# Second layer of a graph-attention kernel: partial sums scaled and added straight from PSUM in chains of multiply-add instructions

## Chip, cores, metric

The kernel runs on one core of a Trainium2 chip. The metric is device time in microseconds. Three runs of the kernel before took 3546.62, 3557.57 and 3558.91 us (median 3557.57). Everything below on single instructions comes from one profiled execution.

## What is computed

Four graph layers follow each other on 3327 nodes with 512 features; each one is `x = x + layer(relu(layernorm(x)), adj)`. The first three are attention layers with 8, 4 and 8 heads, the fourth takes a mean over neighbours. The change concerns the second:

```python
def _L1_gnn_ref(H, A, W, a_l, a_r):
    N_HEADS, D_K = 4, 128
    mask = A + jnp.eye(n, dtype=A.dtype) > 0
    Wh = (H @ W).reshape(n, N_HEADS, D_K)
    sl = jnp.einsum('nhd,hd->nh', Wh, a_l)
    sr = jnp.einsum('nhd,hd->nh', Wh, a_r)
    e = jax.nn.leaky_relu(sl[:, :, None] + sr.T[None, :, :], negative_slope=0.2)
    e = jnp.where(mask[:, None, :], e, -jnp.inf)
    alpha = jnp.nan_to_num(jax.nn.softmax(e, axis=2), nan=0.0)
    out = jnp.einsum('nhm,mhd->nhd', alpha, Wh).reshape(n, -1)
    return jax.nn.elu(out)
```

## The kernel before, in words

**Factored softmax.** exp(leaky_relu(s1 + s2)) is exp(s1)·exp(s2) where s1 + s2 > 0, and exp(0.2·s1)·exp(0.2·s2) elsewhere. So the numerator of a row is `c0 · (T0 @ B0) + c1 · (T1 @ B1)`. T0 and T1 are matrices of 0 and 2 (the neighbours with s1 + s2 > 0, and the others). B0 and B1 are the 128 projected features times the exponential of s2, with the exponential itself as a 129th column (DA = 129) that gives the denominator. c0 and c1 are scales per row and head. They are kept in `L.c` (tile `cpm`), which `close_terms` (lines 562 to 600) computes once a layer from the scores of all nodes: VectorE reductions (568 to 570), a transpose on TensorE (572), a small matmul (579) that hands the maxima to all partitions, a dozen short VectorE instructions (581 to 599), and one exponential on ScalarE (600).

**Pieces.** B is fp32 and is used in pieces along the free axis. For the first of the five groups of source nodes (`JG`: 6, 6, 6, 4 and 4 tiles of 128) these are three bf16 pieces, 387 columns, against the fp8 matrix (line 757). For the other groups there are two fp32r pieces, 258 columns, against a matrix that ScalarE (groups 1 and 2, tile `ts`) or VectorE (groups 3 and 4, tile `tv`) casts to fp32r first (`real`, line 634; matmul line 754). All of them add into one accumulator per row tile: a PSUM bank whose columns 0 to 386 hold three partial sums of 129 columns. Somebody has to add the three.

**Order of the work** (`attention`, lines 680 to 830). The loop goes over chunks of four row tiles (the last has two), heads h, a = 0 and 1 for T0 and T1, and passes. A pass takes two row tiles k over all 26 source tiles j: 52 matmuls. There are four accumulators, two for a pass. In the very first head the passes of a = 0 are cut in two: both pairs over the first 22 source tiles, then both over the last 4, so all four accumulators are full at nearly the same time. When a pass ends, VectorE reads its accumulators (line 775: a reduction that adds the three partial sums of one row tile into R[:, k, a, :]). Then `hooks.run` issues a piece of other work: layer norm, projection and score terms of finished tiles for the next layer. After a = 0 line 789 flips T0 to T1 on VectorE. After both a, VectorE multiplies R by the scales (797), adds the two halves (799), divides (801, 802, 804) and writes the output tile A.

VectorE also makes compares (662), masks (669) and the casts of `tv` for the passes to come. The tile framework places the instructions of each engine in an order of its own, within their dependences; each engine then works through its list strictly in order. Buffers that matter: `acc` 4, `tv` 2, `ts` 3, `tht` 10, R 1.

Of the kernel before, what the change touches and what calls it, by code (L numbers as in the profile page):

```python
# [32 lines left out]
ALU = mybir.AluOpType  # L33
AX = mybir.AxisListType
# [3 lines left out]
P = 128  # L38
# [14 lines left out]
def tile_gnn(ctx: ExitStack, tc: tile.TileContext, x, adj, W0, a01, W1, al, ar, W2, a2,  # L53
             Ws, bs, Wn, bn, Wc, bc, out):
    nc = tc.nc
# [49 lines left out]
    def dims(l):  # L105


        H = heads[l]
        DA = D // H + 1
        AO = -(-(3 * DA + 1) // 8) * 8 if l != 1 else 3 * DA + 1  # L110
        return H, DA, AO, 2 * AO

    abd = []
    for l in range(3):
        H, DA, AO, HW = dims(l)
# [446 lines left out]
    def close_terms(L):  # L562

        l = L.l
        H = heads[l]
        s2v = L.s12[:, 1].rearrange("p t h -> p h t")
        ex = pre.tile([P, 2 * H], F32, name="ex", bufs=1)
        nc.vector.tensor_reduce(ex[:, :H], s2v, AX.X, ALU.max)
        nc.vector.tensor_reduce(ex[:, H:], s2v, AX.X, ALU.min)
        nc.vector.tensor_scalar(ex[:, H:], ex[:, H:], -1.0, None, op0=ALU.mult)  # L570
        tp = ps.tile([2 * H, P], F32, name="tp", bufs=2)
        nc.tensor.transpose(tp, ex, ident)
        m = pre.tile([16, 1], F32, name="mx", bufs=1)
        nc.vector.tensor_reduce(m[:2 * H], tp, AX.X, ALU.max)

        dgm = pre.tile([16, 16], F32, name="dgm", bufs=1)
        nc.vector.tensor_scalar(dgm[:2 * H, :2 * H], ident[:2 * H, :2 * H], m[:2 * H], None, op0=ALU.mult)
        pM = ps.tile([P, 2 * H], F32, name="mm")
        nc.tensor.matmul(pM, ones_row[:2 * H, :], dgm[:2 * H, :2 * H], start=True, stop=True)
        M = pre.tile([P, 2 * H], F32, name="M", bufs=1)  # L580
        nc.vector.tensor_copy(M, pM)
        fl = pre.tile([1, 1], F32, name="fl", bufs=1)
        nc.vector.tensor_reduce(fl, M[0:1, :], AX.X, ALU.max)
        nc.vector.tensor_scalar(fl, fl, S2_MAX, None, op0=ALU.is_gt)
        nc.vector.tensor_max(flagf, flagf, fl)
        L.c = pre.tile([P, NT, 2, H], F32, name="cpm")
        Mb = M[:, None, :H].to_broadcast([P, NT, H])
        s1v = L.s12[:, 0]
        uv = pre.tile([P, D], F32, name="e", bufs=1)
        u, v = [uv[:, o:o + NT * H].rearrange("p (t h) -> p t h", h=H) for o in (0, D // 2)]  # L590
        nc.vector.tensor_scalar(u, Mb, SLOPE, None, op0=ALU.mult)
        nc.vector.tensor_scalar(v, s1v, 1.0 - SLOPE, None, op0=ALU.mult)

        nc.vector.tensor_sub(L.c[:, :, 0, :], v, u)
        nc.vector.scalar_tensor_tensor(L.c[:, :, 0, :], Mb, -1.0, L.c[:, :, 0, :], op0=ALU.mult, op1=ALU.min)

        nc.vector.tensor_add(v, v, Mb)
        nc.vector.tensor_max(v, v, u)
        nc.vector.tensor_scalar(L.c[:, :, 1, :], v, -1.0, None, op0=ALU.mult)
        nc.scalar.activation(L.c, L.c, AF.Exp)  # L600
# [79 lines left out]
    def attention(L, hooks, open_next, close):  # L680

        l = L.l
        H, DA, AO, HW = dims(l)
        DK = DA - 1
        masks = mask_tiles(0, l == 1) if l else masks0
        for c, (t0, nt) in enumerate(chunks):
# [3 lines left out]
            for h in range(H):  # L690
# [10 lines left out]
                for a in range(2 if l == 1 else 1):  # L701
                    row = []
                    for g, (_, nj) in enumerate(JG):
                        if l == 1:
# [3 lines left out]
                            v = (tl if two else tl.bitcast(BF16))[:, :nj * w].rearrange("p (j w) -> p j w", j=nj)  # L708
                            ld = nc.sync.dma_start(v.bitcast(F32) if two else v, abd[l][g][h, a])
                        else:  # L710
                            if g in ahead:
                                v = ahead.pop(g)
                            else:
                                v = pieces_tile(L, mp if l else bp, g)
# [21 lines left out]
                R = mp.tile([P, PER, 2, DA], F32, name="R", bufs=1)  # L736
                deg = l == 0 and h == 0
                for a in range(2 if l == 1 else 1):
                    passes = [(range(k0, min(nt, k0 + 2)), range(NT)) for k0 in range(0, nt, 2)]
                    if c == 0 and h == 0 and a == 0:  # L740
                        cut = JG[-1][0]
                        passes = [(ks, range(0, cut)) for ks, _ in passes] + [(ks, range(cut, NT)) for ks, _ in passes]
                    acc = {}
                    for ks, js in passes:
                        thr = {}
                        for j in js:
                            g, jj = jwhere[j]
                            if l == 1 and KIND[g] != "b" and g not in thr:
                                thr[g] = real(a, g, ks, th)
                            for k in ks:  # L750
                                if j == 0:
                                    acc[k] = accs.tile([P, 512], F32, name="acc")
                                if g in thr:
                                    mm = nc.tensor.matmul(acc[k][:, :2 * DA], thr[g][:, k - ks[0], jj, :], ab[a][g][:, jj, :],  # L754
                                                     start=(j == 0), stop=(j == NT - 1), skip_group_check=True)
                                elif l == 1:
                                    mm = nc.tensor.matmul(acc[k][:, :3 * DA], th[a][g][:, k, jj, :], ab[a][g][:, jj, :3 * DA],  # L757
                                                     start=(j == 0), stop=(j == NT - 1), skip_group_check=True)
                                else:
                                    o = 1 if deg else 0  # L760
                                    nc.tensor.matmul(acc[k][:, :3 * DA + o], th[0][g][:, k, jj, :],  # L761
                                                     ab[0][g][:, jj, :3 * DA + o], start=(j == 0), stop=False,
                                                     skip_group_check=True)
                                    mm = nc.tensor.matmul(acc[k][:, AO:AO + 3 * DA + o], th[1][g][:, k, jj, :],  # L764
                                                     ab[0][g][:, jj, AO:AO + 3 * DA + o], start=False, stop=(j == NT - 1),
                                                     skip_group_check=True)
                            if j == JG[3][0]:
                                late = mm.ins.name
                        if l == 2 and last and h == H - 1:
                            load_y2(yp, 0, late)  # L770
                        if js[-1] != NT - 1:
                            continue
                        for k in ks:
                            if l == 1:
                                nc.vector.tensor_reduce(R[:, k, a, :], acc[k][:, :3 * DA].rearrange("p (s d) -> p d s", s=3),
                                                        AX.X, ALU.add)
                            else:
                                v = acc[k][:, :2 * AO].rearrange("p (a w) -> p a w", a=2)[:, :, :3 * DA]
                                nc.vector.tensor_reduce(R[:, k], v.rearrange("p a (s d) -> p a d s", s=3), AX.X, ALU.add)  # L779
                            if deg:  # L780
                                n = pn(t0 + k)
                                nc.vector.tensor_reduce(deg2[:n, t0 + k:t0 + k + 1],
                                                        acc[k][:n, 3 * DA:AO + 3 * DA + 1:AO], AX.X, ALU.add)
                        gone.append(mm.ins.name)
                        hooks.run(1 if last else 3, hook, 2 if hook % 2 and c == 0 or hook % 3 == 0 and c else 1, 2 if last else 1)
                        hook += 1
                    if a == 0:
                        for pu, mu in flip:
                            nc.vector.tensor_tensor(pu, pu, mu, ALU.bitwise_xor)
                        if h == H - 1 and not last:  # L790
                            pending = loops
                if h == H - 1 and not last:
                    set_loops(pending, gone[-2])
                if c == 0 and h == 0:
                    close_terms(L)
                Rv = R[:, :nt]
                nc.vector.tensor_mul(Rv, Rv, L.c[:, t0:t0 + nt, :, h:h + 1].to_broadcast([P, nt, 2, DA]))
                num = R[:, :, 0, :]
                nc.vector.tensor_add(num[:, :nt], Rv[:, :, 0, :], Rv[:, :, 1, :])
                rc = mp.tile([P, PER, 1], F32, name="rc")  # L800
                nc.vector.tensor_scalar(rc[:, :nt], num[:, :nt, DK:DA], S_MIN, None, op0=ALU.max)  # L801
                nc.vector.reciprocal(rc[:, :nt], rc[:, :nt])
# [90 lines left out]
    with tc.tile_pool(name="first", bufs=1) as fp:  # L893
# [19 lines left out]
        L = open_layer(0)  # L913
# [10 lines left out]
        while hooks.tiles or hooks.flying:  # L924
# [4 lines left out]
            for g in range(3):  # L929
                if n == (8, 15, 21)[g]:  # L930
# [6 lines left out]
                    s = PER * JM * P  # L937
# [5 lines left out]
    A, R = [("A", D, F32, n) for n in A_BUFS], ("R", PER * 2 * 129, F32, 1)  # L943
# [5 lines left out]
    for l in range(3):  # L949
# [17 lines left out]
        L = nxt[0]  # L967
# [12 lines left out]
    with tc.tile_pool(name="agg", bufs=1, reuse_waits="tile") as op:  # L980
# [21 lines left out]
        for c, (t0, nt) in enumerate(chunks):  # L1002
            masks = m0 if c == 0 else mask_tiles(c)
            kss = [range(nt)] if c == 0 else [[k] for k in range(nt)]
            for ks in kss:
                acc = {k: accs.tile([P, 512], F32, name="acc") for k in ks}
# [473 lines left out]
```

## Time and profile before

| what | value |
|---|---|
| median of three runs | 3557.57 us |
| profiled execution | 3569.33 us, its span 3567.4 us |
| granted TensorE clock, mean | 0.987 |
| second layer's matmuls (lines 754, 757) | 1247 to 2092 us of the span |
| line 775, reductions in the second layer | 208, 553 ns on average |
| lines 797 and 799 there, chunks of four row tiles | 24 each, 1333 and 725 ns |

Engines: PE is TensorE's matmuls, PEld its weight loads, DVE VectorE, ACT ScalarE, POOL GpSimd, SP the queue that issues most loads. A group line gives source line, engine, operation, what is written and read, shapes, count, busy time, mean length of one in ns, the engine's idle time in front of them, and what ended it. A line of single instructions gives start, length, engine, line, operation, shapes and count; "x4" is four in a row, merged, and a bracket tells how long the engine idled in front and for whom. A matmul's recorded length includes its way through a pipeline, so the distance from start to start is its price.

### The profile page before, as it was taken

Reading aid. Unit: us, or ns where it says so; the run is one execution under the profiler, and the core shown is the slowest. Engines: PE = TensorE matmul, PEld = TensorE weight load, DVE = VectorE, ACT = ScalarE, POOL = GpSimd, SP = SyncE. Lnnn points to the kernel's source line nnn. Section 1 sums busy time; section 2 is a strip of 40 time slices with the busy share of each in tenths; the row PEclk is TensorE's granted clock in tenths of the full one; section 3 lists DMA queues with packets and bytes.
Section 4 is the critical chain, followed back from the end, with each engine's and each line's share of the span. In section 5 each row is a group of like instructions: output and inputs, shape, how many; then the busy total and the mean of one; then the engine's idle time right before and its main releaser. Section 6 shows DMA issues by size and latency. Waiting matters only on the chain. (4 is left out here: it accounts for less than half of the span.)

```text
span 3567.4 us, 77669 instructions
## 1 busy us (share of the span) xinstructions
PE 3450.4 (97%) x30751; PEld 3112.8 (87%) x30751; DVE 2626.8 (74%) x5227; ACT 2507.5 (70%) x4113; POOL 626.2 (18%) x858
## 2 busy tenths in 40 slices
PE   7899999999999999999999989999999999999999
PEld 6788999999999788888888869989898989876887
DVE  8788887888887689888889868867676768672221
ACT  5777787788788789898888677767666757572111
POOL 6601222112110201223223230101010101020000
PEclk9999999999999999999999999999999999999999
DMA  7799999999957777877777875555555555576331
GB/s 219 217 276 249 217 255 240 250 251 259 269 188 247 260 278 266 288 256 273 282 256 269 319 266 191 192 178 192 172 185 181 174 174 189 163 271 254 116 100 60
DMA packets 398117, 797.70 MB, mean 224 GB/s; under 512 B 112969, under 2 KB 221844, under 8 KB 397104
## 3 DMA queue, kind: packets, MB, share of 16 engines
q1 hardware_dynamic: 363890, 723.14, 63.3%
q0 software_dynamic: 28128, 62.42, 7.5%
q10 hardware_dynamic: 5726, 7.08, 0.7%
q8 instruction: 245, 4.01, 0.5%
q14 instruction: 128, 1.05, 0.1%
HBM read 663.59 MB, written 129.64 MB: 222 GB/s over the span
## 5 line engine op out<-in xcount | busy, mean ns | idle before, releaser
L665 ACT ACTIVATE gt<-s1b,ks 128x512 fp8e4<-128x512 f32 (+1 forms) x2448 | 1448.1, 677 | 280.0 <-issue 150.3
L761 PE MATMUL acc<-ab,tht 128*128 128x195 bf16 (+1 forms) x9112 | 1556.3, 248 | 6.1 <-DVE tht L669 5.3
L764 PE MATMUL acc<-ab,gt 128*128 128x195 bf16 (+1 forms) x9112 | 1555.2, 248 | 5.8 <-DVE rc L801 3.3
L764 PEld LDWEIGHTS <-gt 128*128 128x128 fp8e4 x10744 | 1055.2, 98 | 38.1 <-issue 25.8
L761 PEld LDWEIGHTS <-tht 128*128 128x128 fp8e4 x10744 | 1054.6, 98 | 36.9 <-DVE tht L669 23.3
L669 DVE TENSOR_TENSOR tht<-gt,m 128x768 uint32<-128x768 uint32 (+3 forms) x557 | 448.1, 805 | 136.9 <-ACT gt L665 127.7
L671 DVE TENSOR_TENSOR gt<-tht,m 128x768 uint32<-128x768 uint32 (+3 forms) x557 | 449.9, 808 | 8.5
L634 ACT CAST ts<-tht 128x1536 fp32r<-128x1536 fp8e4 x208 | 300.0, 1469 | 59.9 <-PE acc L754 56.8
L754 PE MATMUL acc<-ab,ts 128*128 128x258 f32 x2496 | 335.4, 290 | 4.6 <-ACT ts L634 2.6
L754 PEld LDWEIGHTS acc<-ab,ts 128*128 128x128 f32 x2496 | 315.0, 191 | 13.9 <-issue 3.6
L1016 PE MATMUL acc<-y,mf 128*128 128x512 f32 x1352 | 309.9, 391 | 3.4 <-DVE mf L1011 3.4
L665 ACT ACTIVATE tht<-s1b,ks 128x512 fp8e4<-128x512 f32 (+1 forms) x504 | 308.3, 680 | 2.7 <-DMA s1b<-s 2.2
L662 DVE TENSOR_SCALAR gt<-s1b,ns 128x512 fp8e4<-128x512 f32 (+1 forms) x446 | 216.0, 491 | 125.7 <-PE acc L764 125.3
L1016 PEld LDWEIGHTS acc<-y,mf 128*128 128x128 f32 x1352 | 253.6, 188 | 59.6 <-DVE mf L1011 3.8
L761 PE MATMUL acc<-abx,tht 128*128 128x195 bf16 (+1 forms) x1632 | 289.0, 250 | 15.0 <-DVE tht L669 14.8
L764 PE MATMUL acc<-abx,gt 128*128 128x195 bf16 (+1 forms) x1632 | 288.5, 250 | 8.4 <-DVE rc L801 3.8
L864 POOL TENSOR_TENSOR xt<-xt,e 128x512 f32<-128x512 f32 x72 | 124.4, 1727 | 907.2 <-DVE e L863 580.5
L779 DVE TENSOR_REDUCE R<-acc 128x130 f32<-128x390 f32 x416 | 214.6, 556 | 82.4 <-PE acc L764 81.8
L757 PE MATMUL acc<-ab,tht 128*128 128x387 bf16 x1248 | 227.5, 331 | 9.3 <-DMA ab<-ab 5.7
L1013 ACT CAST mf<-m 128x768 fp32r<-128x768 fp8e4 (+1 forms) x78 | 59.1, 762 | 246.9 <-PE acc L1016 235.1
L754 PE MATMUL acc<-ab,tv 128*128 128x258 f32 x1664 | 219.0, 283 | 1.4 <-DVE tv L634 1.3
L754 PEld LDWEIGHTS acc<-ab,tv 128*128 128x128 f32 x1664 | 207.5, 190 | 3.0 <-DVE tv L634 2.2
(163 smaller groups left out, 3721.7 us busy)
## 6 DMA issues: line engine op xcount, KB each, us to landing
ab<-ab SPq DMA_DIRECT2D x333, 600.0 KB, 5.5
ab<-ab SPq DMA_DIRECT2D x112, 774.0 KB, 6.4
ab<-ab SPq DMA_DIRECT2D x112, 516.0 KB, 5.2
ab<-ab SPq DMA_DIRECT2D x112, 400.0 KB, 4.0
abx<-ab SPq DMA_DIRECT2D x110, 400.0 KB, 7.9
ab<-ab SPq DMA_DIRECT2D x56, 582.0 KB, 7.0
s1b<-s SPq DMA_DIRECT2D x120, 256.0 KB, 6.2
m<-mask SPq DMA_DIRECT2D x69, 384.0 KB, 4.4
```

The lines of the kernel that those rows point to most:

```text
L634: (nc.scalar.copy if KIND[g] == "s" else nc.vector.tensor_copy)(t[:, :k1 - k0, :nj], th[a][g][:, k0:k1])
L662: nc.vector.tensor_scalar(gv[:, :, jj, :], s1v, L.ns2[:, j, h:h + 1], 2.0, op0=ALU.is_gt, op1=ALU.mult, saturate=False)
L665: nc.scalar.activation(gv[:, :, jj, :], s1v, AF.Relu, bias=L.ks2[:, j, h:h + 1], scale=BIG, saturate=False)
L669: nc.vector.tensor_tensor(pu, gu, mu, ALU.bitwise_and)
L671: nc.vector.tensor_tensor(gu, pu, mu, ALU.bitwise_xor)
L754: mm = nc.tensor.matmul(acc[k][:, :2 * DA], thr[g][:, k - ks[0], jj, :], ab[a][g][:, jj, :], start=(j == 0), stop=(j == NT - 1), skip_grou ...
L757: mm = nc.tensor.matmul(acc[k][:, :3 * DA], th[a][g][:, k, jj, :], ab[a][g][:, jj, :3 * DA], start=(j == 0), stop=(j == NT - 1), skip_grou ...
L761: nc.tensor.matmul(acc[k][:, :3 * DA + o], th[0][g][:, k, jj, :], ab[0][g][:, jj, :3 * DA + o], start=(j == 0), stop=False, skip_group_che ...
L764: mm = nc.tensor.matmul(acc[k][:, AO:AO + 3 * DA + o], th[1][g][:, k, jj, :], ab[0][g][:, jj, AO:AO + 3 * DA + o], start=False, stop=(j == ...
L779: nc.vector.tensor_reduce(R[:, k], v.rearrange("p a (s d) -> p a d s", s=3), AX.X, ALU.add)
L864: nc.gpsimd.tensor_add(xt, xt, e)
L1016: nc.tensor.matmul(acc[k], mf[:, jj, :], y2[g][:, jj, s, :], start=(j0 + jj == 0 and s == 0), stop=(j0 + jj == NT - 1 and s == 1))
```

## The change

In the second layer (l == 1) the reduction of line 775 goes, and so do the multiply (797) and the add (799). In their place every partial sum is read straight from PSUM by an instruction that multiplies it with its row's scale and adds it to R[:, k, 0, :]. The first of a row tile's six only multiplies and writes. The six depend on each other through R: three when a = 0 ends and three when a = 1 ends. Since they need the scales, `close_terms` is called before the first of them, at the end of the first pass of the first head, and no longer at that head's end. The other layers stay as they are.

```diff
                         if js[-1] != NT - 1:
                             continue
+                        if l == 1 and c == 0 and h == 0 and a == 0 and ks[0] == 0:
+                            close_terms(L)
                         for k in ks:
                             if l == 1:
-                                nc.vector.tensor_reduce(R[:, k, a, :], acc[k][:, :3 * DA].rearrange("p (s d) -> p d s", s=3),
-                                                        AX.X, ALU.add)
+
+                                cf = L.c[:, t0 + k, a, h:h + 1]
+                                for s in range(3):
+                                    v = acc[k][:, s * DA:(s + 1) * DA]
+                                    if a == s == 0:
+                                        nc.vector.tensor_scalar(R[:, k, 0, :], v, cf, None, op0=ALU.mult)
+                                    else:
+                                        nc.vector.scalar_tensor_tensor(R[:, k, 0, :], v, cf, R[:, k, 0, :],
+                                                                       op0=ALU.mult, op1=ALU.add)
...
-                if c == 0 and h == 0:
-                    close_terms(L)
-                Rv = R[:, :nt]
-                nc.vector.tensor_mul(Rv, Rv, L.c[:, t0:t0 + nt, :, h:h + 1].to_broadcast([P, nt, 2, DA]))
                 num = R[:, :, 0, :]
-                nc.vector.tensor_add(num[:, :nt], Rv[:, :, 0, :], Rv[:, :, 1, :])
+                if l != 1:
+                    if c == 0 and h == 0:
+                        close_terms(L)
+                    Rv = R[:, :nt]
+                    nc.vector.tensor_mul(Rv, Rv, L.c[:, t0:t0 + nt, :, h:h + 1].to_broadcast([P, nt, 2, DA]))
+                    nc.vector.tensor_add(num[:, :nt], Rv[:, :, 0, :], Rv[:, :, 1, :])
```

In the changed file the new multiply is line 782 and the new multiply-add line 784; lines up to 772 keep their numbers.

## The prediction

> **What bounds the kernel now.** I read the page's head first, then the busy time in stretches of the second layer, then who TensorE waits for there, then the groups of VectorE, and last the single instructions around the places that move. The head:
>
> ```profile
> span 3567.4 us, 77669 instructions
> PE 3450.4 (97%) x30751; PEld 3112.8 (87%) x30751; DVE 2626.8 (74%) x5227; ACT 2507.5 (70%) x4113; POOL 626.2 (18%) x858
> ```
>
> TensorE is busy 97% of the span, VectorE 74%. The change touches the second layer alone, whose matmuls (lines 754 and 757) run from 1247 to 2092 us. Busy time by engine in its start, its steady part and its end:
>
> ```profile
> 1247.00:1290.00 43.00, 42.95 (x279) 34.29 (x280) 36.89 (x77) 42.64 (x61) 3.65 (x8) 1.00 0.78 279
> 1290.00:1990.00 700.00, 693.11 (x5069) 608.29 (x5068) 619.54 (x1138) 597.21 (x792) 173.51 (x181) 1.00 0.76 270
> 1990.00:2095.00 105.00, 94.69 (x612) 79.48 (x611) 76.91 (x167) 67.54 (x117) 33.01 (x43) 0.93 0.92 337
> ```
>
> The columns are stretch, length, PE, PEld, DVE, ACT and POOL busy, granted clock, DMA share and GB/s. In the steady part TensorE is busy 693 of 700 us and VectorE 620 of 700 (88.5%). So VectorE has 80 us to spare, and TensorE has almost nothing to win. The waits of TensorE in the whole layer that VectorE's casts and flips end, and the largest wait of VectorE (waited for: us in total, times, longest):
>
> ```profile
> PE acc L754 <- DVE tv L634: 1.3, 2, 0.7
> PE acc L757 <- DVE tht L789: 0.4, 1, 0.4
> ```
>
> ```profile
> DVE tv L634 <- PE acc L754: 57.7, 27, 5.5
> ```
>
> VectorE runs ahead until it needs a buffer back from TensorE. More work on VectorE is thus free while the spare time lasts.
>
> **What goes and what comes.** The layer has 28 heads of a chunk, 24 with four row tiles and 4 with two, so 26 full ones in effect. Mean ns of one stands behind the busy time:
>
> ```profile
> L775 DVE TENSOR_REDUCE R<-acc 128x129 f32<-128x387 f32 x208 | 106.2, 553 | 9.1 <-PE acc L754 8.3
> L797 DVE TENSOR_TENSOR R<-R,cpm 128x1032 f32<-128x1032 f32 x24 | 32.0, 1333 | 0.0
> L799 DVE TENSOR_TENSOR R<-R 128x516 f32<-128x516 f32 x24 | 17.4, 725 | 0.0
> ```
>
> Records overlap: the next instruction starts some 0.09 us before the last one's record ends. What VectorE pays is start to start. Four L775 in a row take 1.96 us (line in the fence further down), so (1.96 - 0.553)/3 = 0.47 us each. The multiply of line 797 starts at 1292.36 and its successor at 1293.51: 1.15 us. The add of line 799 takes 0.60 (1294.11 to 1294.71). A full head pays 8 x 0.47 + 1.15 + 0.60 = 5.51 us today.
>
> It will pay 24 instructions on 129 columns that read PSUM and take a per-row scalar. None of that size is in the trace. The nearest is line 1025 in the last layer: the same multiply-add, from PSUM, with a per-row scalar, on 512 columns.
>
> ```profile
> 3293.64 0.75 DVE L1025 SCALAR_TENSOR_TENSOR o<-acc,rdeg,y 128x512 f32<-128x512 f32 x1 [0.34 <-PE acc L1016]
> 3294.30 0.42 DVE L1011 CAST mf<-m 128x512 fp32r<-128x512 fp8e4 x1
> ...
> 3295.45 0.75 DVE L1025 SCALAR_TENSOR_TENSOR o<-acc,rdeg,y 128x512 f32<-128x512 f32 x1
> 3296.23 0.69 DVE L1026 SCALAR_TENSOR_TENSOR o<-o,xo 128x512 f32<-128x512 f32 x1
> ```
>
> Before an instruction that does not need its result, 0.66 us start to start; before one that does (line 1026), 0.78. The slope per column comes from L775 (387 columns, 0.47) and L799 (516, 0.60): 0.13/129 = 1.0 ns; L799 to L797 gives 1.07. For 383 columns fewer I take off 0.40. So 0.26 us where the successor is independent, 0.38 where it has to wait. Upper end: all 24 wait, 9.1 us a head, 3.6 more than today, +94 us on VectorE. Lower end: line 804, a multiply by a per-row scalar on 128 columns, of which four in a row take 0.87 us, 0.20 each: 4.8 us a head, -18 us in all. I take 0.26, because in the order of the changed program two row tiles take turns (a, b, a, b, a, b): a step's predecessor started 0.52 before and needs 0.35 (0.75 - 0.40). That makes 24 x 0.26 = 6.24 us a head, +0.73, and 26 x 0.73 = **+19 us on VectorE**, 16 of it in the steady part: 620 becomes 636 of 700 us. The cover is the 58 us that VectorE spends waiting for tv buffers. If it went, the 19 us would be on the path. A pair's eviction grows from 0.94 to 1.56 us; the buffers for the next pair are the other two of four, and a pass of 52 matmuls lasts 6.8 us (1272.34 to 1279.12), so TensorE does not notice. I put down 2 us for passes where VectorE has other work piled up.
>
> [...]
>
> **What moves: close_terms.** It works out the scales (L.c), and the first eviction now waits for it. Before, it was spread over the first head:
>
> ```profile
> 1271.73 1.96 DVE L775 TENSOR_REDUCE R<-acc 128x129 f32<-128x387 f32 x4
> 1272.34 2.14 PE L757 MATMUL acc<-ab,tht 128*128 128x387 bf16 x12
> ...
> 1287.56 0.16 DVE L581 COPY M<-mm 128x8 f32<-128x8 f32 x1
> ...
> 1290.41 0.21 DVE L599 TENSOR_SCALAR cpm<-e 128x104 f32<-128x104 f32 x1
> ...
> 1291.36 0.37 ACT L600 ACTIVATE cpm<-cpm 128x208 f32<-128x208 f32 x1
> ```
>
> In the first head all four accumulators are full when its first half ends; TensorE went on at 1272.34, as soon as the first L775 was through. In the changed order its next pass stands behind the scales. The transpose of line 572 is done by 1271.5. On VectorE: L574 at 1271.73 (0.2), a cast (0.6), L577 (0.07), a cast (0.6) beside the matmul of line 579, L581 at 1273.2. From L581 to the end of L599 took 3.06 us before, with a cast (0.60) and an L669 (0.87) in between; now two L669 and one L662 (0.40) lie there: 3.06 - 0.60 + 0.87 + 0.40 = 3.7, to 1276.9. L600 stands on ScalarE behind ten compares of 0.62 us that began at 1270.96, so it ends near 1277.5. Behind the waiting first multiply on VectorE stand the next head's flips, compares and casts; TensorE needs none of them before it has an accumulator. First multiply 1277.6, third step of its chain 1278.6, done 1279.0. **TensorE goes on at 1279.1 in place of 1272.3: 6.7 us, once.**
>
> A hole has a second price. TensorE stood still from 1313.6 to 1316.6, and then:
>
> ```profile
> 1316.80:1320.20 3.40, 3.40 (x12) 1.61 (x11) 3.40 (x7) 2.16 (x4) 0.00 (x0) 0.51 1.02 421
> ```
>
> Its granted clock was 0.51 for 3.4 us. After the hole from 3145 to 3150 it was 0.50 from 3150.0 to 3156.4. At half clock fourteen L757 took 4.15 us, 0.29 apart, against 0.165 at full clock, so 0.44 of that time is lost: 1.5 to 2.8 us; I take 2.5. Whether the delay swallows the later hole at 1313 (3.0 + 1.5 us) can't be read here: its loads wait in SP's queue for buffers that TensorE frees, so they shift along, and I put it at nothing (bounds -4.5 and 0). The end of the layer loses 0.90 + 0.42 us of multiply and add and gains 6 x 0.26 - 2 x 0.47: under 1 us, beside TensorE's fused weights, nothing. On SP, ScalarE and GpSimd some loads and casts change places by a few positions; each is started earlier than its use by a whole pass, so nothing.
>
> **Sum** against the profiled execution: 3569.3 (span 3567.4) + 6.7 + 2.5 + 2 = 3580.5. It lies 11.8 us above the median 3557.57, so the same +11.2 on the median makes **3568**.
>
> **The rivals.**
> 1. *VectorE becomes the bound* (slower). If each step waits for its predecessor (0.38), the steady part wants 620 + 22 x 3.6 = 699 of 700 us, with waits for TensorE and ScalarE still in the queue. VectorE is a queue in order, so a tv cast comes late and TensorE stops. It decides from about 0.31 us a step, where half of the 80 us is gone. If half of today's 58 us of waiting stays, some +30 on top of 11: near 3597. For it: 88.5% is high, and hooks put 4 us of projection in a clump. Against it: the alternating order, and 1.7 us of TensorE's waits today.
> 2. *The hole is hidden* (no change). If the scales are ready sooner, or the hole at 1313 goes in exchange, 2 to 4 us stay: near 3560.
> 3. *Faster.* The multiply of line 797 took 1.33 us on average against 1.23 undisturbed and at worst 2.08; with it gone, VectorE is steadier. But TensorE's waits in the steady part sum to under 7 us: at best near 3548.
>
> **How the numbers follow.** About 0.5%, 18 us, is what a measurement of this kernel can tell from no change. Forecast 0.57 (own range 3558 to 3580; a seventh of it ends above 3575.4), rival 1 0.23, rival 2 0.16, rival 3 0.04. Slower: 0.23 + 0.08 = 0.31. Rival 3 at its best is 10 us off, so only with the scatter of the runs (3546.62 to 3558.91) does it pass the bound: faster 0.02. The same: 0.67. The range leaves out the top of rival 1 and the bottom of rival 3: 3550 to 3600.
>
> **What would show it.** Line 784 near 0.35 us a record and 0.26 start to start; VectorE's busy time in the steady part near 90 to 91% and TensorE still at 99%; in the first head one hole of 6 to 7 us before the L757 at about 1279, with half clock behind it. I am wrong if the steps cost over 0.31 us start to start, if TensorE's waits for tv grow past 10 us, or if there is no hole at 1272.

## The result and the profile after

The changed kernel took 3578.69 us (median of five runs, 3570.64 to 3582.05) against 3557.57 us before (five runs, 3546.62 to 3561.72). The ratio is 1.0057, with a 95% interval of 1.0039 to 1.0075: 21 us slower, where 11 were forecast. Its profiled execution took 3573.3 us.

The head of its page and the layer's busy time in the stretches of before (stretch, length, PE, PEld, DVE, ACT and POOL busy, granted clock, DMA share, GB/s):

```profile
span 3571.4 us, 78031 instructions
PE 3446.3 (96%) x30751; PEld 3107.2 (87%) x30751; DVE 2637.0 (74%) x5587; ACT 2505.1 (70%) x4113; POOL 642.6 (18%) x858
```

```profile
1247.00:1290.00 43.00, 36.80 (x231) 28.38 (x229) 33.73 (x83) 40.05 (x53) 3.46 (x8) 0.92 0.63 224
1290.00:1990.00 700.00, 692.35 (x5060) 606.94 (x5059) 627.28 (x1441) 587.99 (x779) 195.67 (x177) 1.00 0.76 269
1990.00:2095.00 105.00, 91.79 (x615) 77.72 (x614) 77.79 (x197) 68.14 (x120) 34.61 (x46) 0.97 0.91 334
```

VectorE has 360 instructions more and is 10 us busier over the whole span. In the steady stretch it is busy 627 of 700 us instead of 620, and TensorE still stands at 692. A part of what is lost shows at the start: 36.8 us of TensorE in the first 43 instead of 42.95. The instructions that read PSUM, the cast of `tv`, and how long VectorE still waits for a `tv` buffer:

```profile
L634 DVE CAST tv<-tht 128x1024 fp32r<-128x1024 fp8e4 x208 | 151.4, 731 | 42.6 <-PE acc L754 42.5
L784 DVE SCALAR_TENSOR_TENSOR R<-acc,cpm,R 128x129 f32<-128x129 f32 x520 | 143.9, 343 | 7.3 <-PE acc L754 6.1
L782 DVE TENSOR_SCALAR R<-acc,cpm 128x129 f32<-128x129 f32 x104 | 31.3, 342 | 0.4
```

Its wait before the cast was 57.7 us and is 42.5 now, so most of the new work went into time that VectorE had spent waiting. What TensorE waits for in the layer (line waited for: us in total, times, longest), first in the kernel before, then in the changed one:

```profile
PE acc L757 <- DMA ab<-ab: 5.7, 2, 3.0
PE mm L408 <- ACT hT L142: 1.4, 2, 0.7
```

```profile
PE acc L757 <- DVE R L784: 5.8, 1, 5.8
PE mm L408 <- ACT hT L142: 4.2, 2, 3.6
PE acc L757 <- DMA ab<-ab: 3.8, 2, 2.2
PE acc L754 <- DVE tv L634: 3.7, 13, 0.9
```

Of the changed kernel's, the first line is the forecast hole. The third, for loads of B, is smaller than before (5.7). The other two are not what was forecast: the wait for `hT`, the transposed activations of the next layer's projection, which ScalarE copies (line 142), was 1.4 us in all and 0.7 at the longest, and the wait for `tv` was 1.3 us in 2.

**The first head.** Its single instructions (start, length, engine, line):

```profile
1266.82 0.15 DVE L581 COPY M<-mm 128x8 f32<-128x8 f32 x1
...
1270.16 0.21 DVE L599 TENSOR_SCALAR cpm<-e 128x104 f32<-128x104 f32 x1
...
1270.64 0.36 ACT L600 ACTIVATE cpm<-cpm 128x208 f32<-128x208 f32 x1
...
1271.07 0.61 DVE L782 TENSOR_SCALAR R<-acc,cpm 128x129 f32<-128x129 f32 x2
1271.59 1.12 DVE L784 SCALAR_TENSOR_TENSOR R<-acc,cpm,R 128x129 f32<-128x129 f32 x4
...
1272.51 4.06 PE L757 MATMUL acc<-ab,tht 128*128 128x387 bf16 x12 [5.78 <-DVE R L784]
...
1281.33 1.65 DVE L784 SCALAR_TENSOR_TENSOR R<-acc,cpm,R 128x129 f32<-128x129 f32 x6
```

The layer itself starts 6.45 us earlier here (1240.60 against 1247.05), because the layer ahead of it differs in length from run to run. From the layer's first matmul to this L757 it is 31.9 us; it was 25.3. That is 6.6 us. The last line gives the price of a step: (1.65 - 0.343)/5 = 0.26 us start to start. The clock behind the hole:

```profile
1269.70:1272.50 2.80, 0.00 (x0) 0.00 (x0) 2.80 (x10) 2.80 (x6) 0.00 (x0) 0.50 0.77 321
1272.50:1276.50 4.00, 3.99 (x13) 2.10 (x14) 4.00 (x12) 2.79 (x5) 0.00 (x0) 0.50 0.00 0
```

Half clock from 1269.7 to 1276.5. By the first `tv` matmul of that pass (pass 2 of the table below) the delay is 8.6 us: 6.6 of hole and 2.0 of slow matmuls.

**The layer pass by pass.** The layer before lasts 1068 to 1086 us in the traces of this study, whichever kernel it is, and this scatter covers small effects in a single time. Times counted from the second layer's start are free of it. The following table is worked out from the traces: time from the layer's first matmul to the first `tv` matmul of a pass (of 104, counted from 0), minus the same in the kernel before; the last column is the layer's total up to the third layer's first matmul, 863.2 us before. The runs are told of below.

```
pass                       2     8    26    41    68    98   101   103  | layer
before, again            0.0  -0.3  -0.4   0.1   0.4   0.5   0.4  -1.8  | 861.8
changed                  8.6   7.2   9.4  11.7  13.7  10.6  14.2  12.0  | 876.8
changed, again          10.3   6.4   8.6  10.8  14.8  11.7  17.8  19.1  | 883.9
first head only          8.6   5.2   5.1   6.1   7.5   6.3   6.7   7.1  | 870.3
all but first head       1.6  -2.5   0.5   3.2   5.2   2.3   6.1   4.2  | 869.5
early scales             3.5   2.9   6.0   8.3  12.2   9.0  12.6  10.9  | 876.1
early scales, 2nd run    1.7  -1.6  -0.2   2.1   4.1   1.4   6.7   5.1  | 869.8
early scales, 3rd run    3.4   0.2   1.6   3.9   5.9   3.4   8.0   9.2  | 873.7
early scales, third tv   3.1   3.2   3.9   7.7   8.0   6.3  11.9  11.2  | 876.4
early scales, hT ahead   1.8  -2.2  -0.8   1.5   3.5   0.1   0.5  -1.1  | 863.7
both undone              0.0  -0.6   2.5   5.2   7.1   3.7   4.4   4.2  | 869.0
```

Two traces of the kernel before agree within 0.5 us up to pass 101. Those of one changed kernel agree less: the two of the change within 1.7 us up to pass 98, but they differ by 7.1 at pass 103, and the three of the early scales differ by 8 us at pass 68. A part of this is the clock. Every trace has a pause of TensorE of 2.0 us just before the layer's first matmul. After it, 7 of the 14 traces run for 3.4 us at half clock and the others do not, which makes 1.6 to 1.8 us by pass 2. The changed kernel's second trace is one of them:

```profile
1237.40:1240.80 3.40, 3.40 (x10) 2.51 (x9) 2.18 (x4) 3.40 (x7) 0.00 (x0) 0.50 0.57 222
```

So a single difference shows little; what recurs in all traces of a kind is the kernel's own: a step at the first head, a rise from pass 8 to 68 of which a part is given back by 98, and another between 98 and 101, in the last chunk, where there are only two row tiles. Behind the layer nothing is lost: from the third layer's first matmul to the end the kernel before takes 1457.2 and 1454.7 us in its two traces, the changed one 1454.1 and 1455.1.

### The profile page after: what moved, and what is told of

Its sections match the earlier page's. It is cut to its first block, busy times and chain, and to the rows that moved or that the text cites. A ratio compares the mean times of both kernels' runs of the same rounds, so it can differ in the third digit from the quotient of the medians.

```text
span 3571.4 us, 78031 instructions
## 1 busy us (share of the span) xinstructions
PE 3446.3 (96%) x30751; PEld 3107.2 (87%) x30751; DVE 2637.0 (74%) x5587; ACT 2505.1 (70%) x4113; POOL 642.6 (18%) x858
## 5 line engine op out<-in xcount | busy, mean ns | idle before, releaser
L761 PE MATMUL acc<-abx,tht 128*128 128x195 bf16 (+1 forms) x1632 | 287.6, 249 | 11.2 <-DVE tht L669 10.4
L757 PE MATMUL acc<-ab,tht 128*128 128x387 bf16 x1248 | 229.8, 333 | 13.9 <-DVE R L784 5.8
```

## The experiments

The runs had four accounts of the 21 us to tell apart: the first head, VectorE's load, the late casts of `tv`, and the order of the instructions. The later expectations call the third of these theory C and the fourth theory D. In "microseconds of time" below, a ratio is multiplied by 3560. Each diff is against the changed kernel, and `...` stands for lines not shown.

**1. Chains in all heads but the first.** The first head keeps the reduction, the multiply and the add, and close_terms at its end.

```diff
-                        if l == 1 and c == 0 and h == 0 and a == 0 and ks[0] == 0:
-                            close_terms(L)
                         for k in ks:
-                            if l == 1:
+                            if l == 1 and c + h > 0:
...
+                            elif l == 1:
+                                nc.vector.tensor_reduce(R[:, k, a, :], acc[k][:, :3 * DA].rearrange("p (s d) -> p d s", s=3),
+                                                        AX.X, ALU.add)
...
-                if l != 1:
+                if l != 1 or c + h == 0:
```

> Chains of multiply-adds in 27 of the 28 heads; the first head keeps the reduction, the multiply and the add, and the scales are worked out at its end, as before the change. Theory A (the hole in the first head, 6.6 us and half clock behind it, is the larger single part; the 19 us of extra VectorE work are mostly covered): the hole goes, TensorE passes the first head as before, and some 9 us of the change's 21 go: near 3570. Theory B (the price lies in the other heads, where VectorE comes late): nothing goes, near 3578.

Measured: 3570.84 us, ratio 1.0037 (1.0023 to 1.0051). The hole is gone and 13 us remain (8 to 18).

**2. Chains in the first head only**: the reverse, with close_terms early as in the change.

```diff
-                            if l == 1:
+                            if l == 1 and c + h == 0:
...
+                            elif l == 1:
+                                nc.vector.tensor_reduce(R[:, k, a, :], acc[k][:, :3 * DA].rearrange("p (s d) -> p d s", s=3),
+                                                        AX.X, ALU.add)
...
-                if l != 1:
-                    if c == 0 and h == 0:
+                if l != 1 or c + h > 0:
+                    if l != 1 and c == 0 and h == 0:
                         close_terms(L)
```

> The reverse: the chain and the early scales in the first head alone, the reduction, the multiply and the add in the other 27. Theory A: the hole alone, +9 us on the kernel before, near 3566, with one wait of some 6 us of TensorE before the first pass of the second half and the rest of the layer as before. Theory B: the hole is given back later in the layer by what ran ahead during it, near 3559.

Measured: 3566.91 us, ratio 1.0030 (1.0013 to 1.0046). The wait of 5.8 us for R is back, and TensorE's wait for `hT` is short, 1.0 us at most:

```profile
PE acc L757 <- DVE R L784: 5.8, 1, 5.8
...
PE mm L408 <- ACT hT L142: 2.4, 3, 1.0
```

The parts add up to about the whole: 1.0030 and 1.0037 make 1.0067 against 1.0057 and, in the repeat below, 1.0069. By these times the first head is about half of the price. The other half is in the other heads, where the forecast had put 2 us.

**3. Scales before the first pass.** The whole change, with close_terms called ahead of all passes of the first head:

```diff
+                if l == 1 and c == 0 and h == 0:
+                    close_terms(L)
                 R = mp.tile([P, PER, 2, DA], F32, name="R", bufs=1)
...
-                        if l == 1 and c == 0 and h == 0 and a == 0 and ks[0] == 0:
-                            close_terms(L)
```

> The whole change, but the scales are worked out before the first head's passes (the scores they need are complete when the layer's first matmuls run), so that the first chain finds them ready. Theory A: no hole of TensorE in the first head, near 3570 (as the first experiment), the small matmul and the transpose cost under 1 us. Theory B: near 3578.

Measured: 3573.24 us, ratio 1.0039 (1.0025 to 1.0053). It was run twice more: 3572.18 us, 1.0036 (1.0022 to 1.0050), and 3569.39 us, 1.0029 (1.0012 to 1.0046). TensorE's wait for R shrinks from 5.8 to 0.8 us in all three:

```profile
PE acc L759 <- DVE R L784: 0.8, 1, 0.8
```

So the hole came from where the scales were computed, not from the chains themselves. On the chip where both ran, moving them brought 3579.58 us (ratio 1.0051 to 1.0087) down to 3572.18 (1.0022 to 1.0050). What the second and third run were to show:

> The third experiment once more, beside the third tv buffer on the same chip: 3570 to 3576, no hole in the first head, 10 to 15 waits of TensorE for tv.

> The whole change with the scales closed before the first pass, a third time, for the comparison on the same chip with the run that alters the order. Theory D and the rival alike: 3571 to 3576 us, ratio 1.0035 to 1.0045, a wait for the hT copy of 3.3 to 3.6 us, a second layer of 869 to 876 us in the trace.

**4. One more multiply, and three more,** for each row tile and half, reading the accumulator and writing a part of R that nobody reads: 208 and 624 instructions (`range(3)` in the second), some 54 and 162 us of VectorE at 0.26 each.

```diff
+                                for s in range(1):
+                                    nc.vector.tensor_scalar(R[:, k, 1, :], acc[k][:, s * DA:(s + 1) * DA], cf, None, op0=ALU.mult)
```

> The whole change and, for each row tile and half, one more multiply of 128x129 from PSUM into a half of R that nothing reads: 208 more at 0.26 us start to start, 54 us of VectorE, some 46 of them in the steady part (627 + 46 = 673 of 700 us). Theory A (VectorE's spare time covers it): under +10 us on the changed kernel, 3580 to 3588. Theory B (VectorE is as good as the bound already): half or more of the 54 us show, 3605 or above.

> The whole change and, for each row tile and half, three more multiplies of 128x129 from PSUM into a half of R that nothing reads: 624 more, 162 us of VectorE at 0.26 us each, some 137 of them in the steady part, which then wants 627 + 137 = 764 us in a part that TensorE does in 700. Here VectorE must be the bound whatever the theory: some +75 to +100 us on the changed kernel, near 3660, with TensorE waiting for tv all along. With the run of one more multiply (54 us of VectorE, 3 us of time) this brackets the point from which VectorE decides. If the time rises by under 40 us, the room on VectorE is larger than its busy time tells.

Measured: 3581.92 us, ratio 1.0060 (1.0043 to 1.0076), for one; 3695.97 us, ratio 1.0383 (1.0357 to 1.0410), for three. The steady stretch with one more:

```profile
1290.00:1990.00 700.00, 688.64 (x5042) 604.36 (x5041) 667.85 (x1614) 586.79 (x779) 186.85 (x178) 1.00 0.75 268
```

VectorE is busy 668 of 700 us, 40 more than in the changed kernel, and the time cannot be told from the changed kernel's. (In its trace the layer is 889.3 us long, 5 us more than in the longer of the changed kernel's two, so a few microseconds may be in it.) With three more it has become the bound; the whole layer, and TensorE's waits:

```profile
1238.00:2213.00 975.00, 871.99 (x5946) 741.88 (x5946) 917.21 (x2353) 707.18 (x969) 210.68 (x232) 0.96 0.72 243
```

```profile
PE acc L754 <- DVE tv L634: 36.9, 30, 6.0
PE acc L757 <- DVE R L787: 24.4, 13, 7.1
PE acc L754 <- ACT ts L634: 20.9, 16, 3.5
```

So 10 us more on VectorE are not the price by their amount, and there is an edge further on. This is what rival 1 of the prediction looks like where it is true: TensorE stops behind `tv`, `R` and `ts` alike.

**5. A third tv buffer**, on top of the early scales (R keeps one half in this layer, which makes the room).

```diff
-        t = mp.tile([P, 2, nj, P], F32R, name="ts" if KIND[g] == "s" else "tv", bufs=3 if KIND[g] == "s" else 2)
+        t = mp.tile([P, 2, nj, P], F32R, name="ts" if KIND[g] == "s" else "tv", bufs=3 if KIND[g] == "s" else 3)
...
-                R = mp.tile([P, PER, 2, DA], F32, name="R", bufs=1)
+                R = mp.tile([P, PER, 1 if l == 1 else 2, DA], F32, name="R", bufs=1)
...
```

> The change with early scales (the third experiment, 3573) and three tv buffers in place of two; R has only the half that is used, which makes the room. Theory C (what the 27 other heads cost, 6 to 13 us, is VectorE's cast of tv standing behind a longer eviction in a queue in order, with no spare buffer to cast ahead): TensorE's waits for tv fall from 13 to a few, and the time falls to 3560 to 3566. Theory D (the rest is not a wait for tv): within 3 us of the third experiment, 3570 to 3576.

Measured: 3577.99 us, ratio 1.0053 (1.0035 to 1.0072), beside 1.0036 for the early scales without it on the same chip. All waits for `tv` are gone from the list, which now begins:

```profile
PE acc L759 <- DMA ab<-ab: 5.5, 2, 3.8
PE acc L756 <- DMA ab<-ab: 5.3, 5, 1.9
PE mm L408 <- ACT hT L142: 5.1, 3, 3.7
```

Taking the waits for `tv` away took no time away. From pass 8 to 98 this trace loses 3.1 us, beside 6.1, 3.0 and 3.2 in the three with two buffers. So theory C falls as an account of the price: what TensorE does not wait for there it waits for elsewhere.

**6. The changed kernel again.**

> The changed kernel once more, unchanged, to see how far its time and the length of each layer scatter: 3571 to 3582 as before, with the hole of 6 us in the first head in the same place, and the second layer some 13 us longer than in the kernel before.

Measured: 3579.58 us, ratio 1.0069 (1.0051 to 1.0087). The wait for R is 5.8 us again, that for `hT` 3.4. Its row in the table is a second trace of the same code.

**7. The copy of hT ahead of the compares.** In every kernel with chains in the other heads ScalarE's list in the last chunk differs from before, though no line of ScalarE was edited. Before:

```profile
2025.67 2.83 ACT L634 CAST ts<-tht 128x1536 fp32r<-128x1536 fp8e4 x2
2028.41 0.58 ACT L142 COPY hT<-tp 128x512 f32<-128x512 f32 x1
...
2029.04 3.83 PE L408 MATMUL mm<-w,hT 128*128 128x264 f32 x16 [0.73 <-ACT hT L142]
```

Changed, at the same place:

```profile
2030.88 1.46 ACT L634 CAST ts<-tht 128x1536 fp32r<-128x1536 fp8e4 x1
2031.75 0.60 PE L138 MATMUL tp<-ident,h 128*128 128x128 f32 x4
2032.25 2.10 ACT L665 ACTIVATE tht<-s1b,ks 128x256 fp8e4<-128x256 f32 x5
2034.25 1.45 ACT L634 CAST ts<-tht 128x1536 fp32r<-128x1536 fp8e4 x1
2035.61 0.57 ACT L142 COPY hT<-tp 128x512 f32<-128x512 f32 x1
2036.24 3.83 PE L408 MATMUL mm<-w,hT 128*128 128x264 f32 x16 [3.56 <-ACT hT L142]
```

The transposes (L138) are done at 2032.35, and the copy that TensorE needs next stands behind five compares and a cast: 3.3 us of ScalarE's work. The experiment holds this chunk's compares of group 2 in the third head, and the casts to `ts` from that head on, behind that copy by an ordering hint to the scheduler. It changes nothing else of the early scales:

```diff
+        if hold[0] and KIND[g] == "s":
+            after(cp, hold[0])
...
+                if l == 1 and nt < PER and h == 2 and g == 2:
+                    hold[0] = hold[0] or copied[-2]
+                    after(cp, hold[0])
```

> The early scales of the third and seventh run, and beside them one change of order alone: in the last chunk of rows of the second layer, in its third head, the third group's compares and that head's ts casts on ScalarE are held behind a copy of hT (line 142) that the other kernels with chains run only after them. Nothing is computed differently. Theory D, the price is in the order of instructions: TensorE's wait for the hT copy (3.3 to 3.6 us in every kernel with chains in all heads but the first, 0.7 us before) falls below 1 us, the layer's end is 20.6 us long as before instead of 22, and 2 to 4 us go from the time: 3567 to 3571 us, ratio 1.003 to 1.0035. Rival, the waits only change places: the wait for hT goes, another of 2 to 3 us appears in the same chunk (for a ts cast or a mask), and the time stays at 3571 to 3576 us.

Measured: 3565.56 us, ratio 1.0023 (1.0008 to 1.0037), beside 3569.39 without it on the same chip; those two times alone do not part. The trace does. The wait:

```profile
PE mm L408 <- ACT hT L142: 0.9, 2, 0.7
```

Between passes 98 and 101 the layer now loses 0.4 us. It loses 3.6 to 6.1 in each of the seven traces with chains in all heads, or all but the first, and the other order (8.1 with one more multiply; the kernel with three more, where VectorE is the bound, is left out), and 0.4 with chains in the first head only. The layer is 863.7 us long, as before, and 6 to 12 us shorter than in the three traces of the early scales. Only 3.2 to 4.9 us of this fall between passes 98 and 101; the rest is not shown to come from this edit. The expected shortening of the layer's end, from 22 to 20.6 us, did not come: it is 22.1.

**8. The kernel before, again.**

> The kernel before, once more with its trace, for the scatter of its second layer: if the second layer's 863.2 us is a property of its order of instructions, it is 862 to 865 us here as well, with no wait for the hT copy above 1 us; if the layer scatters as the first one does from run to run (1068 to 1086 us), it can be 870 us as well, and then the differences of 6 to 9 us between the traces show nothing. Time 3550 to 3565 us, ratio 1.0.

Measured: 3558.98 us, ratio 0.9997 (0.9981 to 1.0013). The layer is 861.8 us long, 1.4 less than in the first trace. So the length of this kernel's layer repeats. That of the others repeats less well (876.8 and 883.9 us for the changed kernel, 869.8 to 876.1 for the early scales), and a difference of 6 us between two single layers shows nothing there.

**9. Both places undone**: chains in all heads but the first, and the copy ahead of the compares.

> Chains in all heads of the second layer but the first, as in the first run, and the order of ScalarE's instructions in the last chunk as in the run that held the compares behind the copy of hT; nothing else. If the two places, the first head (8.6 us) and the copy of hT (4 to 6 us), are the whole price, the second layer is 861 to 865 us long as before, and the time 3556 to 3564 us, ratio 0.999 to 1.001. Rival, the chains in the other heads cost something besides, spread over the passes or outside the second layer: the layer is 863 to 868 us, the time 3564 to 3570 us, ratio 1.002 to 1.003, as in the run with the early scales and this order (1.0023).

Measured: 3563.28 us, ratio 1.0007 (0.9985 to 1.0028), and a layer of 869.0 us. TensorE's longest wait for `hT` is 0.7 us, and from pass 98 to 101 the layer loses 0.7. The time speaks for the two places as the whole price, the trace for a rest of 4 us in the passes and 1.5 at the layer's end; the interval is too wide to choose. None of the kernels is faster than the one before.

## Why the prediction was nearly right, and where it was short

The time (3578.69) lies in the range and, by 1.3 us, in the forecast's own range, whose upper seventh is slower by over 0.5%. The sign and the main mechanism of the forecast were right; its rise was half the measured one. That the time falls inside the forecast's own range is partly luck: the repeat's ratio of 1.0069 would be 3582 us here, above it. And by the prediction's chances a change too small to tell (0.67) was likelier than a slower kernel (0.31). The last step of its sum is rounded down: 3557.57 and 11.2 make 3568.8. By its steps, with the changed kernel's first trace and then its second:

- *The step costs 0.26 us, and VectorE covers it.* Right: 0.26 start to start and 0.343 a record. VectorE's busy time rose by 8 us in the steady part, not 16, and by 10 over the span.
- *The hole: 6.7 us and 2.5 for the clock.* Right: 6.6 and 2.0 in the first trace. In the second the layer is 10.3 us late at the same pass, and 1.7 of them come from the half clock at the layer's start. L581 to the end of L599 took 3.55 us, forecast 3.7.
- *The hole at 1313, put at nothing (bounds -4.5 and 0).* From pass 2 to 8 the kernel gets 1.4 us back, and 3.9 in the second trace: the wait for a load there was 3.0 us before and is 1.6 and 0.8. The delay is not needed for it, as the kernel with chains in all heads but the first has no hole and gets 4.1 back (a wait of 0.2).
- *2 us for passes with work piled up.* Too small. From pass 8 to 68 the kernel loses 6.5 us (8.4), and has 3.1 of it back by pass 98: in part because the kernel before waits there too (between 1760 and 1890 us 1.3 us for `tv`, 1.0 for a load and 0.4 for a flip). Net 3.4 (5.3). One case is to be seen below. The late casts alone are not the cause: without any (fifth experiment) the net loss was 3.1 us. What it is was not settled.
- *"On SP, ScalarE and GpSimd some loads and casts change places by a few positions; each is started earlier than its use by a whole pass, so nothing."* **This step failed.** It was argued for loads and casts, none of which a run tested singly, and taken for everything on these engines. The copy of `hT` is used by the next matmul on TensorE's list, 0.06 us after it ends; a few positions on ScalarE are 3.3 us of TensorE. Price 3.6 us (6.1); with the copy put ahead, in the seventh experiment, 0.4.
- *The layer's end, nothing.* 1.5 us more from its last matmul to the third layer's first (22.1 against 20.6; 1.6 in the second trace). No run settled why.

With -2.2 and +1.3 us between passes 101 and 103, where the kernel before differs by 2.2 between its own two traces, this makes 13.6 us in the first trace and 20.7 in the second; the times say 21 and 25, with intervals from 14 to 27 and from 18 to 31. None of the prediction's signs of being wrong appeared (0.26 us a step, 3.7 us of waits for `tv`, a hole): they watched VectorE, and none watched ScalarE's order.

A late cast of `tv` in the changed kernel:

```profile
1676.05 1.12 DVE L784 SCALAR_TENSOR_TENSOR R<-acc,cpm,R 128x129 f32<-128x129 f32 x4
...
1677.09 1.28 DVE L445 TENSOR_TENSOR AB<-mm,AB 128x512 f32<-128x512 f32 x2
...
1678.28 0.69 DVE L634 CAST tv<-tht 128x1024 fp32r<-128x1024 fp8e4 x1
...
1679.03 1.23 PE L754 MATMUL acc<-ab,tv 128*128 128x258 f32 x8 [0.92 <-DVE tv L634]
```

The eviction chain, then two adds of projected features, then the cast, and TensorE 0.92 us late. The mean load is 90%, but here everything stands in one clump.

*Rival 1* (VectorE the bound) is refuted for this change: 40 us more in the steady part did not move the time by what can be told. Over 22 heads of 24 steps that is 0.08 us a step, so the point from which it decides, put at 0.31 us, is nearer to 0.34 or beyond it, as an estimate. *Rival 2* (the hole hidden) did not happen by itself, and the third experiment shows how it is done. *Rival 3* has nothing for it.

What stays open: whether the chains in the other heads cost anything in time beyond the copy of `hT`. The traces say up to 6 us (both places undone: 869.0 us). From pass 8 to 98 the nine traces with chains there and no added multiplies lose 2.3 to 6.1 us, against 0.8 in the kernel before, run again, and 1.1 with chains in the first head only. The times of experiments 7 and 9, 1.0023 and 1.0007, hold both answers.

## What to carry to other kernels

Where a scheduler places instructions, an edit on one engine can reorder another one's list. Don't judge the moved instructions as a class: for each, ask how long after its end its user starts. Those with a whole pass of slack were put at nothing here, which no run tested singly; the copy between two steps of the same chain made TensorE wait 3.56 us, behind 3.3 us of ScalarE's work. And when an instruction is moved so that it needs an early result, move the making of that result earlier as well: calling close_terms ahead of the passes took the wait from 5.8 to 0.8 us.

## What the hardware showed

**Nearly equal waits, unequal clocks.** In the changed kernel TensorE waited 3.56 us for `hT` and went on at full clock; in its repeat it waited 3.38 us, and the granted clock fell:

```profile
2036.00:2040.00 4.00, 3.76 (x17) 3.15 (x18) 2.39 (x9) 1.00 (x2) 2.56 (x4) 1.00 0.26 101
```

```profile
2033.90:2040.50 6.60, 6.60 (x18) 5.03 (x19) 2.12 (x8) 0.81 (x1) 3.49 (x5) 0.57 0.45 141
```

The sixteen matmuls of L408 took 3.83 us in the first and 6.60 in the second. So the same place cost the layer 3.6 us in one and 6.1 in the other, and not by the length of the wait. In five other traces with a wait of about this length, the same sixteen took 3.83 us after waits of 3.55 and 3.41, and 5.51, 5.52 and 5.51 after waits of 3.35, 3.28 and 3.72. The pause of 2.0 us at the layer's start was followed by half clock in 7 of the 14 traces and by full clock in the other 7. So neither at 2.0 us nor at 3.3 to 3.7 us did the length of the wait part the two cases, and what does, no run here shows.

**A load of 95% was nearly free.** VectorE at 668 of 700 us cost nothing that the times show; at 917 of 975, with 624 instructions more, the time rose by 116 us over the changed kernel on the same chip. The share alone does not tell the two apart. This is the stretch from 1290 to 1990 us with three more multiplies:

```profile
1290.00:1990.00 700.00, 633.30 (x4382) 540.86 (x4380) 669.61 (x1703) 511.01 (x673) 142.76 (x152) 0.96 0.70 237
```

VectorE is busy for 670 us here too, but TensorE for 633 instead of 689.
